# Layer 0 attention: position biases from coefficients and one-hot keys, weighted sums one unit later, short and long products interleaved

## The chip, the cores and the metric

The kernel runs on one core of a Trainium2 chip. The core has a matrix engine (TensorE; PE in the profile, with its weight loads listed as PEld), a vector engine (VectorE, DVE), a scalar engine (ScalarE, ACT), GpSimd (POOL) and SyncE (SP, which issues most transfers). PE writes only to PSUM, which here is eight banks of 128 partitions by 512 float32 numbers. The metric is device time in microseconds (us) of one execution; the time before is 5272.12 us, the median of three runs between 5258.96 and 5286.7.

## The reference

Input x has two images of 128 channels by 256 x 256 pixels, all float32. Two residual layers follow each other, each on group-normalised input (32 groups).

Layer 0 is a halo attention. q, k and v are 1 x 1 convolutions of the normalised x. The image is cut into 32 x 32 windows of 8 x 8 queries; keys and values come from the 12 x 12 pixels around the window. There are 4 heads of 32 channels. The part that the change is about is the position bias and the mask:

```
attn = einsum('bnd,bmd->bnm', q, k) + rel_pos_emb(q, rel_height, rel_width) + FIXED_MASK
attn = softmax(attn); out = einsum('bnm,bmd->bnd', attn, v); x = x + W_out(out)
```

rel_pos_emb is the product of a query with a table row that depends on the horizontal distance to the key, plus the product with one that depends on the vertical distance. FIXED_MASK is minus infinity wherever the horizontal or the vertical distance has the wrong parity, so a query sees only the 6 x 6 keys of its 12 x 12 that match in the parity of row and column.

Layer 1 is a convolution block (a 5 x 1 full convolution, a 3 x 1 depthwise one, a product with a small 1 x 3 dilated one). The change does not touch it.

## The kernel before

`attention_fast` does layer 0, `convolutions_fast` layer 1. Because of the mask the kernel splits pixels by parity. A strip k is eight image rows of one image (64 strips: 2 images x 32), a unit u = 2k + r is one row parity r of a strip (128 units). Within a unit c is the column parity. A unit has 16 pairs of neighbouring windows per column parity; a pair n has 32 queries, and its keys are ten columns by six rows, 60 keys, of which the left window uses the first six columns and the right window the last six.

A unit does this, with the functions' names and lines:

- `normalise(k)` (L199): once per strip, for the next strip: POOL copies two carried rows (L213), DVE normalises two halves into the tile f_xn (L220), in two alternating buffers.
- `queries` (L244): two products of 512 columns into a bank of the two-bank pool f_pj, copied out by ACT to f_q (L253). `keys` (L227): the same into f_kt (L240), with a POOL copy of two carried rows (L232).
- `values` (L255): for four groups j of four pairs, eight products of 128 x 60 weights (60 cells of f_xn) by 128 columns into one f_pj bank; two copies each to f_vt (L268), on DVE but for two of the eight, which go to ACT. f_vt has a 33rd column of ones, for the denominators.
- `scores` (L273): in four banks, one per head. Eight lanes (4 heads x 2 column parities) are 32-row by 60-column pieces of the array. Per lane come 8 products with f_rw (horizontal table, one per query column v; 64 columns each), 4 with f_rh (vertical, one per query row t; 128 columns) and 16 with f_kt (one per pair; 32 columns). All are issued through one helper, L286.
- `numerators` (L302): eight ACT exponentials of 256 columns (L307), two per head, with the mask of a window as bias.
- `attend(u, half)` (L313): 64 products per half, of 60 x 32 weights (numerators) by 33 columns (values), into the banks f_o. `head_outputs` (L327): DVE reciprocals (L332), scaling (L333), transpose (L337).
- `project(u, half)` (L340): one product of 512 columns, two DVE additions of x (L350); after the second half a POOL transfer to memory (L356) and two statistics for layer 1 (L93).

PE's order is written out by hand (the block `manual_schedule`). For each unit it is: scores(u), values(u+1), project(u-1, both halves), attend(u, 0), queries(u+1), keys(u+1), attend(u, 1). The other engines' orders are set by a planner from dependencies. Each float32 product shows in the profile as two LDWEIGHTS and two MATMUL records, so a unit's 224 + 32 + 2 + 128 + 4 = 390 products are 780 MATMUL records.

The reciprocals of the whole layer are kept in `rc_all` (4096 numbers per partition), and `in_range` (L556) takes their largest and smallest after layer 0, to choose a slower fallback if a denominator is out of range. The fallback doesn't run here.

Of the kernel before, what the change touches and what calls it, by code (L numbers as in the profile page):

```python
# [18 lines left out]
P = 128  # L19
W = 256  # L20
HEADS = 4
# [5 lines left out]
XC = 130  # L27
XW = 272

DEN_LOW, DEN_HIGH = 1.0e-24, 1.0e36  # L30

# [14 lines left out]
def host_constants():  # L46
# [16 lines left out]
    mask = np.full((2, 64, 2), NEG, np.float32)  # L63
    for key in range(60):
        c = key // 6
        mask[:, key, 0] = 0.0 if c < 6 else NEG
        mask[:, key, 1] = 0.0 if c >= 4 else NEG

    sel = np.zeros((4, 32, P), np.float32)
    for ch in range(P):  # L70
# [7 lines left out]
        "c_mask": mask.reshape(P, 2),  # L78
# [48 lines left out]
def attention_fast(tc, io, x1_d, norm, st_x, st_y, tags, rc_all):  # L127
# [6 lines left out]
    with ExitStack() as l0:  # L134
# [12 lines left out]
        mask = cload("mask", io["c_mask"], [P, 2])  # L147
        rw = cload("rw", io["rw"], [P, 8, 60])
        rh = cload("rh", io["rh"], [P, 4, 60])
# [13 lines left out]
        sc = [ps_s.tile([P, 512], F32, tag=f"s{h}", name=f"f_s{h}") for h in range(HEADS)]  # L163
        for i in range(2):
            nc.gpsimd.memset(xn[i], 0.0)
            for r in range(2):
                nc.gpsimd.memset(kt[r][i], 0.0)
            nc.gpsimd.memset(vt[i], 1.0)
        for h in range(HEADS):
            nc.vector.memset(sc[h], 0.0)  # L170

        with ExitStack() as setup:
            sp = setup.enter_context(tc.tile_pool(name="f_setup", bufs=6))
            for s in range(NS):
                t = sp.tile([P, 8, W], F32, tag="sx", name=f"f_sx_0_{s}")
                nc.sync.dma_start(t, x[0, :, 8 * s : 8 * s + 8, :])
                norm.chunk(st_x[0], 4 * s, t)
# [5 lines left out]
        raws, norms, qs, pts, ots, x1s, po = {}, {}, {}, {}, {}, {}, {}  # L183
# [43 lines left out]
        def keys(u):  # L227
            k, r = divmod(u, 2)
            s = k % NS
            cur, prev, xt = kt[r][k % 2], kt[r][(k + 1) % 2], xn[k % 2]  # L230
            if s > 0:
                nc.gpsimd.tensor_copy(cur[:, :, :, 0:2], prev[:, :, :, 4:6])  # L232
            for c in range(2):
                for lo, hi in ((0, 2), (2, 6)) if s == 0 else ((2, 6),):
                    n = hi - lo
                    pk = ps_pj.tile([P, 512], F32, tag="pj", name=f"f_pk_{u}_{c}_{lo}")
                    nc.tensor.matmul(  # L237
                        pk[:, : n * P], wkT, xt[:, r, c, 1:129, lo:hi], start=True, stop=True
                    )
                    nc.scalar.copy(  # L240
                        cur[:, c, 1:129, lo:hi], pk[:, : n * P].rearrange("p (j i) -> p j i", i=n)
                    )

        def queries(u):  # L244
# [3 lines left out]
            for c in range(2):  # L248
# [6 lines left out]
        def values(u):  # L255
            k, r = divmod(u, 2)
            xt = xn[k % 2]
            for j in range(4):
                pv = ps_pj.tile([P, 512], F32, tag="pj", name=f"f_pv_{u}_{j}")
                for n in range(4):  # L260
                    for c in range(2):
                        col = 8 * (4 * j + n)
                        nc.tensor.matmul(  # L263
                            pv[64 * c : 64 * c + 60, P * n : P * n + P],
                            xt[:, r, c, col : col + 10].rearrange("p j i -> p (j i)"), wvT, start=True, stop=True,
                        )
                for c in range(2):
                    (nc.scalar.copy if c and j > 1 else nc.vector.tensor_copy)(  # L268
                        vt[u % 2][64 * c : 64 * c + 60, 4 * j : 4 * j + 4, :, 0:32],
                        pv[64 * c : 64 * c + 60].rearrange("p (n h d) -> p n h d", n=4, h=HEADS),  # L270
                    )

        def scores(u):  # L273
            k, r = divmod(u, 2)
            q = qs.pop(u).rearrange("p c (n v t) -> p c n v t", n=NPAIR, v=8)
            lanes = [(h, c) for h in range(HEADS) for c in range(2)]

            def lane(h, c):
                return (
                    sc[h][64 * c : 64 * c + 60].rearrange("p (n v t) -> p n v t", n=NPAIR, v=8),  # L280
                    q[32 * h : 32 * h + 32, c],
                    slice(32 * h, 32 * h + 32),
                )

            def mm(out, w, m, start, stop):
                nc.tensor.matmul(out, w, m, start=start, stop=stop, skip_group_check=True)  # L286

            for v in range(8):
                for h, c in lanes:
                    o, m, rows = lane(h, c)  # L290
                    mm(o[:, :, v], rw[rows, v, :], m[:, :, v], v == 0, False)
            for t in range(4):
                for h, c in lanes:
                    o, m, rows = lane(h, c)
                    mm(o[:, :, :, t], rh[rows, t, :], m[:, :, :, t], False, False)
            for n in range(NPAIR):
                for h, c in lanes:
                    o, m, rows = lane(h, c)
                    keys_n = kt[r][k % 2][rows, c, 8 * n : 8 * n + 10].rearrange("p j i -> p (j i)")
                    mm(o[:, n], keys_n, m[:, n], False, n == NPAIR - 1)  # L300

        def numerators(u):  # L302
            p = wk.tile([P, HEADS, 512], F32, tag="p", name=f"f_p_{u}")
            pts[u] = p
            for h in range(HEADS):
                for e in range(2):
                    nc.scalar.activation(  # L307
                        p[:, h].rearrange("p (n e q) -> p n e q", e=2, q=16)[:, :, e],
                        sc[h].rearrange("p (n e q) -> p n e q", e=2, q=16)[:, :, e],
                        AF.Exp, bias=mask[:, e : e + 1],  # L310
                    )

        def attend(u, half):  # L313
            for c in range(2):
                po[c] = ps_o.tile([P, 8, 33], F32, tag=f"o{c}", name=f"f_o_{u}_{half}_{c}")
            p, v = pts[u], vt[u % 2]
            for n in range(8):
                m = 8 * half + n
                for c in range(2):
                    rows = slice(64 * c, 64 * c + 60)  # L320
                    for h in range(HEADS):
# [3 lines left out]
                        )  # L325

        def head_outputs(u, half):  # L327

            on = wk.tile([P, 2, 8, 32], F32, tag="on", name=f"f_on_{u}_{half}")
            for c in range(2):  # L330
                rc = rc_all[:, 2 * (2 * u + half) + c]
# [4 lines left out]
            ot = wk.tile([P, 512], F32, tag=f"ot{half}", name=f"f_ot_{u}_{half}")  # L336
            nc.vector.transpose(ot, on.rearrange("p c n d -> p (c n d)"))  # L337
            ots[u, half] = ot

# [20 lines left out]

        load_rows(0)
        load_rows(1)
        with tc.manual_schedule(engines={PE}):
            normalise(0)
            keys(0)
            queries(0)
            values(0)
            for u in range(NU + 1):
                k, r = divmod(u, 2)
                b, s = divmod(k, NS)  # L370
                if u < NU:
                    if r == 0:
                        if k + 2 < NB * NS:
                            load_rows(k + 2)
                        if k + 1 < NB * NS:
                            normalise(k + 1)
                    scores(u)
                    numerators(u)
                    if b + 1 < NB and s + 1 < NS:
                        stats_chunk(b + 1, 2 * s + r)  # L380
                        if u < 2:
                            stats_chunk(b + 1, 2 * NS - 2 + u)
                if u + 1 < NU:
                    values(u + 1)
                if u > 0:
                    project(u - 1, 0)
                    project(u - 1, 1)
                if u < NU:
                    attend(u, 0)
                    head_outputs(u, 0)  # L390
                    if u + 1 < NU:
                        queries(u + 1)
                        keys(u + 1)
                    attend(u, 1)
                    head_outputs(u, 1)
                    del pts[u]
# [133 lines left out]
def kernel_body(tc, io, out):  # L530
# [3 lines left out]
    with ExitStack() as ctx:  # L534
# [12 lines left out]
        rc_all = glob.tile([P, 8 * NB * NS, 8, 1], F32, tag="rc_all", name="rc_all")  # L547
        attention_fast(tc, io, x1_d, norm, st_x, st_y, tags, rc_all)
        good = in_range(tc, glob, rc_all)
# [6 lines left out]
def in_range(tc, glob, rc_all):  # L556

    nc = tc.nc
    with ExitStack() as ctx:
        sp = ctx.enter_context(tc.tile_pool(name="f_range", bufs=1))  # L560
        ps = ctx.enter_context(tc.tile_pool(name="f_range_ps", bufs=1, space=PSUM))
        flat = rc_all.rearrange("p a b c -> p (a b c)")
        ends = sp.tile([P, 2], F32, tag="ends", name="ends")
        nc.vector.tensor_reduce(ends[:, 0:1], flat, AX.X, ALU.max)
        nc.vector.tensor_reduce(ends[:, 1:2], flat, AX.X, ALU.min)
        nc.vector.tensor_scalar(ends[:, 0:1], ends[:, 0:1], 1.0 / DEN_LOW, None, ALU.is_le)
        nc.vector.tensor_scalar(ends[:, 1:2], ends[:, 1:2], 1.0 / DEN_HIGH, None, ALU.is_ge)
# [571 lines left out]
```

## Time and profile before

| what | us |
|---|---|
| median of three runs | 5272.12 |
| profiled execution, its own time | 5269.7 |
| its span, first to last instruction | 5267.7 |
| PE, records' busy time (share of the span) | 4224.9 (80%) |
| DVE / ACT / POOL busy | 2252.3 / 1168.6 / 785.9 |
| first and last start of a score product (L286) | 110.4 and 3843.2 |
| layer 1 | about 3880 to the end |

The page of the profile gives one execution. The busy share is a union of records: a matmul's record covers more time than it keeps the array, so PE is not working at its peak when it is busy. The granted clock is the share of PE's full clock that was let through. The groups of instructions say for each line how often, how long, and how long the engine was idle just before and what ended that idleness; "issue" there is time in which the engine waited for nothing that the profile shows.

### The profile page before, as it was taken

The page shows a single profiled execution, that of the slowest core. Times are in us where ns is not written, and L with a number is a line of the kernel's source. Part 1 is how long each engine was busy: PE and PEld are TensorE (multiplying, and loading weights), DVE is VectorE, ACT ScalarE, POOL GpSimd, SP SyncE. Part 2 cuts the span into 40 slices and gives each one's busy share as a digit, 9 for nine tenths or more (in the row PEclk, how much of TensorE's full clock was granted, in tenths as well). Part 3 has the DMA queues.
Part 4 walks back from the last instruction along what each step waited for, and adds up shares of the span by engine and source line. Part 5 has one row for each costly group of instructions (what it writes and reads, how often), then busy time and mean ns, then how long its engine had stood idle before and what let it go on. Part 6 is the DMA issues. An engine that isn't in the chain of part 4 may idle for free. (4 is left out here: it accounts for less than half of the span.)

```text
span 5267.7 us, 218868 instructions
## 1 busy us (share of the span) xinstructions
PE 4224.9 (80%) x104494; PEld 2681.7 (51%) x104494; DVE 2252.3 (43%) x3705; ACT 1168.6 (22%) x2197; POOL 785.9 (15%) x656
## 2 busy tenths in 40 slices
PE   2777777777777777777777777777779999999998
PEld 1555555555555555555555555555533333333333
DVE  8754343333433343334343333344344444444443
ACT  0222222222222222222222222222212222222221
POOL 1000000000000000000000000000023333333333
PEclk9777877787777787877778777877789999999999
DMA  8531111111111111111111111111022222222221
GB/s 337 187 110 40 43 41 52 39 43 39 54 39 44 37 53 39 43 39 53 39 43 40 53 39 43 39 53 40 21 75 97 105 102 96 96 96 98 106 99 70
DMA packets 71458, 367.06 MB, mean 70 GB/s; under 512 B 8224, under 2 KB 8992, under 8 KB 50080
## 3 DMA queue, kind: packets, MB, share of 16 engines
q1 hardware_dynamic: 42912, 218.74, 12.7%
q0 software_dynamic: 27648, 134.23, 6.2%
q8 instruction: 822, 13.47, 1.1%
q14 instruction: 76, 0.62, 0.0%
HBM read 218.72 MB, written 134.22 MB: 67 GB/s over the span
## 5 line engine op out<-in xcount | busy, mean ns | idle before, releaser
L268 DVE COPY f_vt<-f_pv 60x512 f32<-60x512 f32 x768 | 527.4, 687 | 1768.3 <-PE f_pv L263 1759.4
L490 PE MATMUL a<-xm,w 128*128 128x512 f32 (+1 forms) x2560 | 1128.6, 594 | 0.0
L286 PE MATMUL f_s<-f_q,f_kt 32*60 32x32 f32 x32768 | 526.2, 265 | 381.3 <-issue 381.3
L263 PE MATMUL f_pv<-f_wqkvT,f_xn 128*60 128x128 f32 x8192 | 767.5, 359 | 64.6 <-DVE f_vt L268 49.2
L490 PEld LDWEIGHTS a<-xm,w 128*128 128x128 f32 x2560 | 471.2, 188 | 653.6 <-issue 653.0
L307 ACT ACTIVATE f_p<-f_s,f_mask 128x256 f32<-128x256 f32 x1024 | 388.1, 488 | 1826.0 <-PE f_s L286 1826.0
L263 PEld LDWEIGHTS f_pv<-f_wqkvT,f_xn 128*60 128x60 f32 x8192 | 675.2, 184 | 134.2 <-PE f_pv L263 72.5
L286 PEld LDWEIGHTS f_s<-f_q,f_kt 32*60 32x60 f32 x32768 | 501.5, 176 | 414.5 <-issue 414.0
L509 DVE SCALAR_TENSOR_TENSOR t<-t,w,t 128x2048 f32<-128x2048 f32 x128 | 323.2, 2525 | 751.0 <-ACT t L494 738.7
L356 POOL DMA_DIRECT2D f_x<-f_x x128 | 91.3, 713 | 2991.5 <-DVE f_x L350 2991.5
L286 PE MATMUL f_s<-f_q,f_rw 32*60 32x64 f32 x16384 | 266.3, 260 | 297.9 <-issue 297.9
L322 PEld LDWEIGHTS f_o<-f_vt,f_p 60*32 60x32 f32 x32768 | 303.2, 105 | 237.3 <-issue 137.8
L286 PEld LDWEIGHTS f_s<-f_q,f_rw 32*60 32x60 f32 x16384 | 226.9, 151 | 321.7 <-issue 316.4
L286 PE MATMUL f_s<-f_q,f_rh 32*60 32x128 f32 x8192 | 315.6, 407 | 70.3 <-issue 70.3
L322 PE MATMUL f_o<-f_vt,f_p 60*32 60x33 f32 x32768 | 334.5, 201 | 41.0 <-issue 39.3
L494 ACT COPY t<-a 128x512 f32<-128x512 f32 (+1 forms) x256 | 149.4, 583 | 900.6 <-PE a L490 880.2
L347 PE MATMUL f_py<-f_ot,f_woT 128*128 128x512 f32 x512 | 286.8, 651 | 46.6 <-ACT f_vt L268 35.8
L286 PEld LDWEIGHTS f_s<-f_q,f_rh 32*60 32x60 f32 x8192 | 234.9, 180 | 98.7 <-issue 97.9
L237 PE MATMUL f_pk<-f_xn,f_wqkvT 128*128 128x512 f32 (+1 forms) x528 | 266.4, 625 | 4.4 <-issue 3.1
L350 DVE TENSOR_TENSOR f_x<-f_py,f_raw 128x256 f32<-128x256 f32 x512 | 193.5, 420 | 154.0 <-PE f_py L347 152.7
L268 ACT COPY f_vt<-f_pv 60x512 f32<-60x512 f32 x256 | 148.6, 580 | 488.4 <-DVE f_vt L268 488.4
L253 ACT COPY f_q<-f_pq 128x512 f32<-128x512 f32 x256 | 149.8, 586 | 477.3 <-PE f_pq L250 477.3
(93 smaller groups left out, 3122.5 us busy)
## 6 DMA issues: line engine op xcount, KB each, us to landing
f_raw<-in_x SPq DMA_DIRECT2D x62, 1280.0 KB, 6.8
f_x<-f_x POOLq DMA_DIRECT2D x128, 512.0 KB, 5.3
out<-y POOLq DMA_DIRECT2D x64, 1024.0 KB, 4.5
raw<-f_x SPq DMA_DIRECT2D x64, 640.0 KB, 4.2
f_sx<-in_x SPq DMA_DIRECT2D x32, 1024.0 KB, 12.2
f_sx<-in_x SPq DMA_DIRECT2D x64, 512.0 KB, 3.8
raw<-f_x SPq DMA_DIRECT2D x62, 384.0 KB, 4.8
f_raw<-in_x SPq DMA_DIRECT2D x2, 1024.0 KB, 5.7
```

Source lines behind the costliest of these rows:

```text
L237: nc.tensor.matmul(pk[:, : n * P], wkT, xt[:, r, c, 1:129, lo:hi], start=True, stop=True)
L253: nc.scalar.copy(q[:, c, :], pq)
L263: nc.tensor.matmul(pv[64 * c : 64 * c + 60, P * n : P * n + P], xt[:, r, c, col : col + 10].rearrange("p j i -> p (j i)"), wvT, start=True ...
L268: (nc.scalar.copy if c and j > 1 else nc.vector.tensor_copy)(vt[u % 2][64 * c : 64 * c + 60, 4 * j : 4 * j + 4, :, 0:32], pv[64 * c : 64 * ...
L286: nc.tensor.matmul(out, w, m, start=start, stop=stop, skip_group_check=True)
L307: nc.scalar.activation(p[:, h].rearrange("p (n e q) -> p n e q", e=2, q=16)[:, :, e], sc[h].rearrange("p (n e q) -> p n e q", e=2, q=16)[: ...
L322: nc.tensor.matmul(po[c][32 * h : 32 * h + 32, n, :], p[rows, h, 32 * m : 32 * m + 32], v[rows, m, h, :], start=True, stop=True,)
L347: nc.tensor.matmul(py, woT, ots.pop((u, half)), start=True, stop=True)
L350: nc.vector.tensor_tensor(x1[:, :, cols], py[:, 256 * c : 256 * c + 256].rearrange("p (m t) -> p t m", t=4), raws[k][:, r:8:2, cols], ALU.add,
L490: nc.tensor.matmul(pa[:, : n * W], w1[:, tap, :], xt[:, j - 2 + tap : j - 2 + tap + n, 2 : 2 + W], start=tap == 0, stop=tap == 4,)
L494: nc.scalar.copy(t1[:, j : j + n, :].rearrange("p r w -> p (r w)"), pa[:, : n * W])
L509: nc.vector.scalar_tensor_tensor(t3, t1[:, tap : tap + 8, :], w3[:, tap : tap + 1], t3, ALU.mult, ALU.add)
```

## The change

- **Biases.** The tables f_rw and f_rh go. Instead a product per query position (t2, t1) of the strip computes, straight from f_xn, for each head 18 numbers per query: its product with the six or twelve rows of the tables that its keys can need. The weights `wb` for this are made once, from W_q and the tables (`g_rel`). ACT copies the numbers to the tile f_cf, and with them two numbers per query that select its window's mask. Then one product per head and column parity, with the constant one-hot weights `hot` (32 x 64) and 512 columns of f_cf, adds to every score the horizontal term, the vertical term and the mask. So 8 products of 512 columns per unit (`biases`) and 16 products of 128 columns per strip (`coefficients`) stand where 96 products per unit of 64 or 128 columns stood.
- **Exponentials.** The mask is in the scores, so `numerators` goes: four exponentials of 512 columns per unit.
- **Sixty-four keys.** Score and value products take 64 cells instead of 60 (the last four are masked), XC grows to 131, and a value group is copied in one instruction of 128 partitions, always by ACT.
- **Order.** The weighted sums of unit u-1 are now computed during unit u, and the projections follow them. `scores` is split by heads in two passes of 16 parts of 4 products; `values`, `attend`, `coefficients` return lists of parts too, and `merge` lays a list of parts of long products between the parts of short ones. In a unit: biases, scores of heads 0 and 1 with values group 0 and the next unit's queries between them; attend half 0 of u-1 with a projection, values group 1 and coefficients; scores of heads 2 and 3 with values group 2 and keys; attend half 1 with a projection, values group 3 and coefficients.
- **Range check.** Largest and smallest reciprocal are taken per strip, so the two reductions over 4096 numbers become 128 over 64 numbers and two over 64.

```diff
+    hot = np.zeros((HEADS, 32, 64), np.float32)
+    for key in range(64):
+        j, i = divmod(key, 6)
...
+        hot[:, 18, key] = 0.0 if j < 6 else NEG
+        hot[:, 19, key] = 0.0 if 4 <= j < 10 else NEG
...
-        rw = cload("rw", io["rw"], [P, 8, 60])
-        rh = cload("rh", io["rh"], [P, 4, 60])
+        hot = cload("hot", io["c_hot"], [P, 64])
+        keep = cload("keep", io["c_keep"], [P, 4])
...
+        def coefficients(k, t2):
+            if t2 == 0:
+                cfs[k] = wk.tile([P, 2, 2, 512], F32, tag="cf", name=f"f_cf_{k}")
+            cf = cfs[k].rearrange("p r c (n e b t) -> p e b t (r c n)", e=2, b=4, t=4)
+            bank = []
+            def part(t1):
+                if t1 == 0:
+                    bank.append(ps_pj.tile([P, 512], F32, tag="pj", name=f"f_pa_{k}_{t2}"))
+                pa = bank[0]
+                nc.tensor.matmul(
+                    pa[:, P * t1 : P * t1 + P], wb[:, t2, t1].rearrange("p h x -> p (h x)"),
+                    xn[k % 2][:, :, :, 1 + t2 : 129 : 4, 1 + t1], start=True, stop=True,
+                )
+                if t1 == 3:
+                    for e in range(2):
+                        nc.scalar.activation(
+                            cf[:, e, t2], pa.rearrange("p (t m e) -> p e t m", t=4, e=2)[:, e],
+                            AF.Identity, bias=keep[:, 2 * e + 1 : 2 * e + 2],
+                            scale=keep[:, 2 * e : 2 * e + 1],
+                        )
+            return [lambda t=t: part(t) for t in range(4)]
...
+        def biases(u):
+            k, r = divmod(u, 2)
+            for h in range(HEADS):
+                rows = slice(32 * h, 32 * h + 32)
+                for c in range(2):
+                    nc.tensor.matmul(
+                        sc[h][64 * c : 64 * c + 64, :], hot[rows, :], cfs[k][rows, r, c, :],
+                        start=True, stop=False, skip_group_check=True,
+                    )
...
+            def part(n):
+                for h in heads:
+                    rows = slice(32 * h, 32 * h + 32)
+                    for c in range(2):
                         nc.tensor.matmul(
+                            sc[h][64 * c : 64 * c + 64, 32 * n : 32 * n + 32],
+                            keys_k[rows, c, 48 * n : 48 * n + 64], qs[u][rows, c, 32 * n : 32 * n + 32],
+                            start=False, stop=n == NPAIR - 1, skip_group_check=True,
                         )
...
+                if n == NPAIR - 1:
...
+                    for h in heads:
+                        nc.scalar.activation(pts[u][:, h], sc[h], AF.Exp)
...
+        def merge(small, large):
+            done = 0
+            for i, f in enumerate(small):
+                f()
+                upto = (i + 1) * len(large) // len(small)
+                for g in large[done:upto]:
+                    g()
+                done = upto
+            for g in large[done:]:
+                g()
...
-                    scores(u)
-                    numerators(u)
...
+                if now:
+                    biases(u)
+                    merge(scores(u, 0), values(u, 0) + (queries(u + 1) if u + 1 < NU else []))
+                merge(
+                    attend(u - 1, 0) if last else [],
+                    ([lambda: project(u - 2, 1)] if u > 1 else []) + (values(u, 1) if now else [])
+                    + (coefficients(k + 1, 2 * r) if more else []),
+                )
+                if now:
+                    merge(scores(u, 1), values(u, 2) + (keys(u + 1) if u + 1 < NU else []))
+                    del qs[u]
+                merge(
+                    attend(u - 1, 1) if last else [],
+                    ([lambda: project(u - 1, 0)] if last else []) + (values(u, 3) if now else [])
+                    + (coefficients(k + 1, 2 * r + 1) if more else []),
+                )
...
-        flat = rc_all.rearrange("p a b c -> p (a b c)")
...
+        nc.vector.tensor_reduce(span[:, 0:1], ends[:, 0, :], AX.X, ALU.max)
+        nc.vector.tensor_reduce(span[:, 1:2], ends[:, 1, :], AX.X, ALU.min)
```

## The prediction

> **What bounds the kernel now.** I read the page first (busy shares, slices, queues), then the waits between 500 and 3700 us, then one unit in the timeline, then that unit by stages.
>
> ```profile
> PE 4224.9 (80%) x104494; PEld 2681.7 (51%) x104494; DVE 2252.3 (43%) x3705; ACT 1168.6 (22%) x2197; POOL 785.9 (15%) x656
> PEclk9777877787777787877778777877789999999999
> q8 instruction: 822, 13.47, 1.1%
> ...
> PE f_s L286 <- issue: 637.7, 382, 4.3
> PE f_o L322 <- issue: 39.3, 15, 4.6
> PE f_pv L263 <- DVE f_vt L268: 34.1, 88, 0.6
> ```
>
> PE is busiest, no other engine is near half. In layer 0 its clock is 0.7 to 0.8, in layer 1 full. Between 500 and 3700 us, some 110 units, its long waits end with "issue": no engine and no transfer is waited for. The queue line says what it is. 822 fetches of 16.4 KB (13.47 MB / 822) carry the 209 thousand PE instructions, one per 254. The single records agree: in the score stage PE stops after every 256 instructions, 1.4 to 2.3 us each time. Example: a fetch starts at 2002.36, takes 1.31 us, and PE resumes at 2005.04; the next one starts 1.1 us after that. So a new block of 256 cannot be had sooner than about 3.5 us after the last one was entered, and PE waits where it eats a block faster.
>
> ```profile
> 2032.43 1.86 PE L286 MATMUL f_s<-f_q,f_rw 32*60 32x64 f32 x103 [2.06 <-issue]
> ...
> 2039.64 1.99 PE L286 MATMUL f_s<-f_q,f_kt 32*60 32x32 f32 x128 [0.71 <-issue]
> 2043.12 0.89 PE L286 MATMUL f_s<-f_q,f_kt 32*60 32x32 f32 x42 [1.48 <-issue]
> 2043.94 6.35 PE L263 MATMUL f_pv<-f_wqkvT,f_xn 128*60 128x128 f32 x64
> 2050.70 2.16 PE L347 MATMUL f_py<-f_ot,f_woT 128*128 128x512 f32 x4 [0.41 <-ACT f_vt L268]
> 2052.79 1.29 PE L322 MATMUL f_o<-f_vt,f_p 60*32 60x33 f32 x128
> 2054.01 1.99 PE L250 MATMUL f_pq<-f_xn,f_wq_s 128*128 128x512 f32 x4
> 2055.87 2.02 PE L237 MATMUL f_pk<-f_xn,f_wqkvT 128*128 128x512 f32 x4
> 2057.82 1.29 PE L322 MATMUL f_o<-f_vt,f_p 60*32 60x33 f32 x128
> ```
>
> The bracket is the idle time before a row: 128 records (256 instructions with their weight loads) last 2 us and then PE stands still. The long products have no such gap.
>
> ```profile
> 2029.90:2043.90 14.00, 8.70 (x458) 7.80 (x448) 3.38 (x7) 0.00 (x0) 0.85 (x1) 0.57 0.02 5
> 2043.90:2050.70 6.80, 6.39 (x70) 5.69 (x64) 3.81 (x6) 3.60 (x9) 0.00 (x0) 0.63 0.01 2
> 2050.70:2052.80 2.10, 2.10 (x6) 0.61 (x6) 1.07 (x3) 0.58 (x1) 0.00 (x0) 1.00 0.00 0
> 2052.80:2054.00 1.20, 1.20 (x129) 1.16 (x128) 1.07 (x3) 0.00 (x0) 0.05 (x1) 1.00 0.05 14
> 2054.00:2057.80 3.80, 3.80 (x16) 1.34 (x8) 2.58 (x7) 1.76 (x3) 0.66 (x1) 1.00 0.34 138
> 2057.80:2059.00 1.20, 1.20 (x129) 1.18 (x128) 0.00 (x0) 0.61 (x1) 0.41 (x1) 1.00 0.05 14
> ```
>
> Stages of one unit: scores, values, projection, attend, queries and keys, attend; after the length the busy times of PE, PEld, DVE, ACT and POOL, then the clock. A unit lasts 29.1 us. Scores take half of it with PE idle 38% of the time, and the clock falls to half there; the values that follow start at half clock, though they never pause. Value records start 55 ns apart at full clock and 107 at half.
>
> **The change, part by part, per unit, on PE's path.** I add what each part will take at full clock, from the starts of single records.
>
> Handovers come first, as the new order is made of them. Before, groups of different array shape meet six times a unit; after, 56 times (merge lays 6, 9, 6, 9 long parts among 16, 8, 16, 8 short ones; neighbours of one kind join). Long to short: the last 512-column record starts 0.53 us before the first attend record, and 0.43 of that is its own stream, so 0.10. Short to long: 0.123 us from the last attend record to the first query record; 0.213 from the last score record to the first value record, seen at half clock only. Between 0.12 and 0.21 I take 0.17 for scores.
>
> - Biases: the 96 products with f_rw and f_rh (192 records) go. Eight products of 512 columns come, 16 records of 0.43 us over eight lanes. The f_rw records at full clock start 7 to 10 ns apart, where one such stream is 53 ns, so eight lanes do run side by side: 2 x 0.43, 0.95 with fill (1.8 if only four do).
> - Scores: 256 records as before, but a pass has two heads, four lanes. A lane repeats every 0.100 us at half clock (its 60-column weight load), so 0.053 at full. A block of three parts, six records per lane, takes 0.05 + 5 x 0.053 + 0.17 = 0.50; one of two parts 0.39. Eight and four of them: 5.6 (4.9 to 6.2). That is more than the 2.5 of 256 records at 9.7 ns in one go.
> - Values: 16 parts of four records, starts spread over 0.163, then 0.107 + 0.10 to hand over: 0.37 each, 5.9 (5.1 to 6.7); 6.8 now.
> - Attend: 16 parts of 16 records, spread 0.093 to 0.12, plus 0.123: 0.24 each, 3.8 (3.5 to 4.3); 2.4 now.
> - Queries, keys, projections: six products, 2 x 0.43 + 0.10 = 0.96 each, 5.8; 5.9 now.
> - Coefficients, new: eight products of 128 columns. Two records of 0.107, and a handover of 0.10: 0.31. They read every 24th number of f_xn; f_rh, which reads every fourth, starts 28.5 ns apart at both clocks, that is 0.228 per record and lane, so up to 0.55. I take 0.40: 3.2 (2.5 to 4.4).
>
> Sum 0.95 + 5.6 + 5.9 + 3.8 + 5.8 + 3.2 = 25.3 us against 29.1.
>
> Fetching: 310 products are 1240 instructions, 4.84 blocks where 390 made 6.1; at 3.5 us that is 17 us, below 25. The densest stretch, scores with values, has 56 instructions in 0.87 us, a block in 4.0 us, so the 6.3 us of issue waits per unit (637.7 + 39.3 + 11.6 over 110) should go. If the parts were faster than I think, 17 plus the 5.8 of the 24 instructions that are nearly free of fetching, 22.4, is a floor.
>
> The Trainium skill, "Runtime: NRT & Kernel Launch", Instruction fetch mechanics, says that crossing a 16 KiB boundary is mostly hidden. By that rule the 6.3 us of pauses would have another cause and would stay, and the unit would take 25.3 + 6.3 = 31.6 us, 5580 in all; the trace shows them at every 256th instruction, and the sum goes by the trace.
>
> The clock: layer 0 stands at 0.79 from 500 to 3700 us. It falls in stretches with pauses (0.57 in the scores, PE busy 8.70 of 14.00) and stands at 1.00 in the attend stages, short records without pauses, and in the long products. The new unit has long products every microsecond and no pause over 0.2, so I take full clock.
>
> The Trainium skill, "TensorE: Matmul & The Clock Gate", Part 1, puts the half clock after an idle window of some 3.4 us. The waits here are mostly 1 to 2 us and the clock falls all the same; by the page's rule pauses of this length cost no clock, filling them would win none, and with today's share of half clock the unit would take 30.6 us.
>
> What lies beside PE:
>
> - ACT now per unit: exponentials four of 512 (eight of 0.38 were 3.0; now 2.4 to 3.0), copies of q, k and values 8 x 0.59 = 4.7, coefficients 4 x 0.48 = 1.9: about 9.5 of 25. The tightest place: the second query copy stands behind two exponentials, ready 1.2 us after its product; values group 1 needs that bank 1.4 us after. If that slips, 0.5 us twice a unit. Should the new function need table loads among the exponentials, four of 1.28 us fit into ACT's free time.
> - DVE loses six copies (4.1 us). normalise now waits for values of the unit before (f_xn's buffer is read longer), 2.7 us of DVE; coefficients need it only after the first score pass, some 7 us later. Behind it on DVE stand the projection's additions, whose bank is free for 2.4 us more.
> - POOL and SP: same transfers in the loop; rows are loaded two strips ahead. At the start 360 KB of tables go and about 120 KB come, under 1 us at 337 GB/s. wb's fill (POOL) and 36 small ACT copies lie beside 98 us of DVE statistics.
> - Ends: the two reductions over 4096 (4.4 us each) stand before layer 1 and go: -8.8. Unit 0 has no attend, the last one's follow after the loop as now; the first coefficients replace the first values. Together about -10.
>
> Total: 5269.7 - 128 x 3.8 - 10 = 4773; the profiled execution stands 2.4 below the median. Predicted 4770.
>
> **Rivals.**
>
> - *Half clock stays (slower).* Array streams double, handovers partly: biases 1.8, scores 8, values 7.5, attend 4.5, long products 10.8, coefficients 5, so about 38. With a share h of half clock a unit takes 25.3 + 12.7 h; it is slower from h = 0.30, and with today's 0.42 it is 30.6, 5450 us. For it: scores with array pieces of 32 rows are weak work, and handovers leave the array empty for some 6 us a unit. Against: the attend stages keep full clock.
> - *Handovers cost more.* At 0.40 a pair instead of 0.25, 28 x 0.15 = 4.2 eats all the gain: 29.5, 5310. Nothing in the trace shows pieces as short as these. It decides at 0.39 a pair.
> - *Fetch or bank waits remain*, two us a unit: 5030.
> - *Everything at its low end*, the fetch floor of 22.4: 4400.
> - *The change does nothing:* PE bound by fetching with the same blocks. The block count alone falls by a fifth; I give it little.
>
> **How the numbers follow.** Forecast (4590 to 4960) 0.47; low ends 0.13; remaining waits (up to 5245) 0.16; within 0.5% (26 us, about what a measurement here can tell from nothing) 0.03; the two slower rivals together 0.21. Range: 4430 leaves out about 0.06 below, 5400 some 0.12 above.
>
> **What would show it.** Right: no "issue" row over 100 us in the waits of 500 to 3700, clock above 0.95 there, a unit (one distance of equal records) of 24 to 27 us, no table loads in the loop. Wrong: clock still at 0.8; value parts more than 0.45 us long; PE waiting for f_pv or f_pq copies by ACT, or for f_cf; score rows with issue gaps.

## The result and the profile after

The changed kernel takes 6282.45 us (median of four runs, 6263.94 to 6296.79) against 5271.61 for the kernel before: 1.191 times as long, 95% interval 1.187 to 1.196. The forecast was 4770 with a range of 4430 to 5400, so it has the wrong sign and the time lies outside the range.

The page of the profile after (busy shares, clock by slices, queues) and the waits of PE from 500 to 4500 us:

```profile
span 6261.9 us, 177334 instructions
PE 6036.0 (96%) x84022; PEld 3082.1 (49%) x84022; DVE 1792.6 (29%) x3061; ACT 1535.1 (25%) x2493; POOL 740.6 (12%) x657
PEclk8777776677767676677677767767777999999999
q8 instruction: 661, 10.83, 0.7%
...
PE f_s L352 <- ACT f_cf L316: 74.8, 52, 1.5
PE pv_x L127 <- DVE q_x L125: 1.3, 1, 1.3
PE f_pv L335 <- DVE f_x L431: 0.7, 1, 0.7
PE f_s L367 <- issue: 0.5, 1, 0.5
```

The first things to see are what came true. PE is busy 96% of the span; the "issue" wait of the score products went from 637.7 us (500 to 3700) to 0.5 (500 to 4500); the fetches fell from 822 to 661. And still the kernel is 1000 us slower. What is left to explain it stands in the clock row: in layer 0 the digits are 6 and 7 where they were 7 and 8. Layer 1 still has nines and lasts as long as before (1420 us from the start of the last score record to the end of the span, 1424 before).

The timeline of PE over the second half of one unit and the start of the next, and the three stages that it runs through (length, then busy times of PE, PEld, DVE, ACT and POOL, then the clock):

```profile
2510.24 0.29 PE L392 MATMUL f_o<-f_vt,f_p 64*32 64x33 f32 x16
2510.46 0.84 PE L310 MATMUL f_pa<-f_xn,f_wb 128*128 128x128 f32 x2
2511.23 0.29 PE L392 MATMUL f_o<-f_vt,f_p 64*32 64x33 f32 x16
...
2512.45 1.46 PE L310 MATMUL f_pa<-f_xn,f_wb 128*128 128x128 f32 x4
...
2515.37 0.70 PE L335 MATMUL f_pv<-f_wqkvT,f_xn 128*64 128x128 f32 x4
2516.00 0.65 PE L367 MATMUL f_s<-f_q,f_kt 32*64 32x32 f32 x16
...
2522.46 2.07 PE L273 MATMUL f_pk<-f_xn,f_wqkvT 128*128 128x512 f32 x2
...
2513.80:2525.90 12.10, 12.10 (x154) 6.71 (x153) 0.50 (x1) 3.98 (x8) 0.00 (x0) 0.58 0.01 1
2525.90:2533.10 7.20, 7.20 (x155) 3.88 (x154) 1.99 (x8) 1.38 (x3) 0.65 (x1) 1.00 0.02 5
2533.10:2541.10 8.00, 8.00 (x183) 4.62 (x182) 0.61 (x2) 3.98 (x7) 0.00 (x0) 1.00 0.01 2
```

A coefficient product (f_pa, two records of 128 columns) holds PE 0.77 us from its start to the next short part, more than twice a value part, though it has half its records. Behind the coefficients comes the score pass, and the first one of the three stages, a pass of heads 2 and 3 with values and keys, ran at a clock of 0.58 and took 12.1 us; the pass of heads 0 and 1 of the next unit found full clock and took 7.1, biases included (2533.14 to 2540.25; the third window runs on into the next stage). There is no pause in either.

Adding up single records from 500 to 4500 us (one unit is 37.2 us there) gives each part's time, at full clock and as it ran:

| part, per unit | forecast | at full clock | as it ran |
|---|---|---|---|
| biases | 0.95 | 0.91 | 1.52 |
| scores, 8 blocks of three and 4 of two | 5.6 | 5.30 | 7.77 |
| values, 16 | 5.9 | 5.90 | 7.62 |
| attend, 16 | 3.8 | 3.57 | 3.69 |
| queries, keys, projections, 6 | 5.8 | 6.34 | 9.98 |
| coefficients, 8 | 3.2 | 5.85 | 6.59 |
| sum | 25.3 | 27.9 | 37.2 |

The unit of 37.2 us is the distance from the first score record to the last, divided by 127. "At full clock" is the number of parts times the median of those that ran wholly at full clock. The third column has 8.6 us more from half clock and 0.7 of waiting for f_cf (in the coefficients' row). So the handovers were priced well, the coefficients were not, and the clock does most of the rest.

### The profile page after: what moved, and what is told of

Same layout as the page of the kernel before. It is cut to its first block, busy times and chain, and to the rows that moved or that the text cites. A ratio compares the mean times of both kernels' runs of the same rounds, so it can differ in the third digit from the quotient of the medians.

```text
span 6261.9 us, 177334 instructions
## 1 busy us (share of the span) xinstructions
PE 6036.0 (96%) x84022; PEld 3082.1 (49%) x84022; DVE 1792.6 (29%) x3061; ACT 1535.1 (25%) x2493; POOL 740.6 (12%) x657
## 5 line engine op out<-in xcount | busy, mean ns | idle before, releaser
L367 PEld LDWEIGHTS f_s<-f_q,f_kt 32*64 32x64 f32 x32768 | 930.0, 193 | 830.1 <-issue 830.0
L335 PE MATMUL f_pv<-f_wqkvT,f_xn 128*64 128x128 f32 x8192 | 1119.6, 361 | 0.7 <-DVE f_x L431 0.7
L367 PE MATMUL f_s<-f_q,f_kt 32*64 32x32 f32 x32768 | 1100.3, 274 | 0.5 <-issue 0.5
L392 PEld LDWEIGHTS f_o<-f_vt,f_p 64*32 64x32 f32 x32768 | 380.2, 109 | 1015.3 <-issue 1013.5
L310 PE MATMUL f_pa<-f_xn,f_wb 128*128 128x128 f32 x2048 | 802.7, 515 | 0.0
L392 PE MATMUL f_o<-f_vt,f_p 64*32 64x33 f32 x32768 | 610.8, 209 | 3.8 <-issue 3.2
L335 PEld LDWEIGHTS f_pv<-f_wqkvT,f_xn 128*64 128x64 f32 x8192 | 489.9, 164 | 107.8 <-issue 2.7
L316 ACT ACTIVATE f_cf<-f_pa,f_keep 128x256 f32<-128x256 f32 x512 | 343.3, 769 | 753.5 <-PE f_pa L310 753.5
L292 PE MATMUL f_pq<-f_xn,f_wq_s 128*128 128x512 f32 x512 | 414.7, 902 | 0.0
L310 PEld LDWEIGHTS f_pa<-f_xn,f_wb 128*128 128x128 f32 x2048 | 363.7, 209 | 61.7 <-ACT f_q L295 0.6
```

What stands on the lines that cost most here:

```text
L292: nc.tensor.matmul(pq, wq_s, xn[k % 2][:, r, c, 1:129, 1:5], start=True, stop=True)
L310: nc.tensor.matmul(pa[:, P * t1 : P * t1 + P], wb[:, t2, t1].rearrange("p h x -> p (h x)"), xn[k % 2][:, :, :, 1 + t2 : 129 : 4, 1 + t1], ...
L316: nc.scalar.activation(cf[:, e, t2], pa.rearrange("p (t m e) -> p e t m", t=4, e=2)[:, e], AF.Identity, bias=keep[:, 2 * e + 1 : 2 * e + 2 ...
L335: nc.tensor.matmul(pv[64 * c : 64 * c + 64, P * n : P * n + P], xt[:, r, c, o : o + 64], wvT, start=True, stop=True,)
L367: nc.tensor.matmul(sc[h][64 * c : 64 * c + 64, 32 * n : 32 * n + 32], keys_k[rows, c, 48 * n : 48 * n + 64], qs[u][rows, c, 32 * n : 32 * ...
L392: nc.tensor.matmul(po[c][32 * h : 32 * h + 32, n, :], p[rows, h, 32 * m : 32 * m + 32], v[rows, m, h, :], start=True, stop=True,)
```

## The experiments

The first theory was "clock": score passes with only short pieces and value parts are too weak to hold full clock. The rival was "handovers": 56 changes of array shape a unit cost more than they seemed. Clock below is the granted clock from 500 to 3000 us.

| run | time, us | ratio to before | unit, us | clock | coefficient record to next, us |
|---|---|---|---|---|---|
| before | 5271.61 | | 29.4 | 0.78 | |
| changed kernel | 6282.45 | 1.191 | 37.2 | 0.71 | 0.307 |
| e1 spread order | 6191.02 | 1.177 | 36.7 | 0.71 | 0.307 |
| e2 grouped order | 5370.96 | 1.021 | 30.2 | 0.80 | 0.307 |
| e3 products added | 7388.18 | 1.404 | 46.1 | 0.67 | 0.307 |
| e4 contiguous copy | 5235.87 | 0.995 | 29.3 | 0.89 | 0.112 |
| e5 copy, 16 bytes apart | 5866.00 | 1.117 | 33.8 | 0.79 | 0.228 |
| e6 contiguous, spread | 5130.38 | 0.977 | 28.4 | 0.89 | 0.112 |
| e7 contiguous, grouped | 4768.17 | 0.908 | 25.5 | 0.90 | 0.112 |
| e8 contiguous, spread, runs of four | 4582.75 | 0.873 | 24.1 | 0.96 | 0.112 |
| e9 contiguous, each product twice | 5345.87 | 1.009 | 30.0 | 0.93 | 0.112 |
| e10 as e8, without the copy | 5246.10 | 0.991 | 29.2 | 0.85 | 0.307 |
| e11 as e8, coefficients first | 4472.79 | 0.845 | 23.2 | 0.98 | 0.112 |

Ratios are against runs of the kernel before made beside each kernel; its medians there lie between 5248.70 and 5294.89. Unit is the distance from the first score record to the last, divided by 127.

**e1, order of the long parts.**

```diff
+        def spread(v, full):
+            if len(full) != 2:
+                return full + v
+            return [full[0], v[0], v[1], full[1], v[2], v[3]]
...
-                    merge(scores(u, 0), values(u, 0) + (queries(u + 1) if u + 1 < NU else []))
+                    merge(scores(u, 0), spread(values(u, 0), queries(u + 1) if u + 1 < NU else []))
...
-                    merge(scores(u, 1), values(u, 2) + (keys(u + 1) if u + 1 < NU else []))
+                    merge(scores(u, 1), spread(values(u, 2), keys(u + 1) if u + 1 < NU else []))
```

> The changed kernel with one edit of order: in the two score passes of a unit the long parts stand as query, value, value, query, value, value (and so with keys) where they stood as four values and then two queries. Same products, same 56 handovers. Theory 'clock': the changed kernel's parts add up to 28 us a unit at full clock and it takes 37 because the score passes with only values in them are too weak to hold the clock; a query product in every 3 us lifts them, the share of half clock from 500 to 4500 us falls from 0.58 to under 0.25, and the time to 5200-5600. Rival 'handovers': the short pieces cost this whatever their neighbours, time stays at 6280 within 60.

6191.02 us, ratio 1.177 (1.173 to 1.181), clock 0.71 as before the edit. Neither came out: the time fell by 90 us, not by 700, and the clock did not come back. So a score pass that begins with four value parts and no query or key product isn't what drops it.

**e2, no interleaving.**

```diff
-                upto = (i + 1) * len(large) // len(small)
+                upto = 0
```

> The changed kernel with merge laying all short parts first and the long ones behind them: 56 handovers a unit become 8. Theory 'handovers': some 48 x 0.2 to 0.27 us of a unit go, 37 becomes 24 to 27, 4650-5000. Theory 'clock': 48 handovers at full clock are worth 6 us, but passes of 256 instructions in a row bring pauses for instructions back (up to 1.8 us, three or four times a unit) and with them some half clock: 26 to 31 us a unit, 4900-5500, issue waits over 200 us.

5370.96 us, ratio 1.021 (1.018 to 1.024): 7.0 us a unit less than the changed kernel, inside the range that "clock" had given; but issue waits stayed at 12 us, far below the 200 expected. Instead the coefficient products wait for the copies of the values, 156.4 us between 500 and 3700, some 1.5 a unit. The clock rose to 0.80. Interleaving so finely costs more than the pauses that it hides, but handovers and clock change together here, and the run doesn't separate them.

**e3, strong products added to the score passes.**

```diff
                 pv = bank[0]
+                for e in range(2 if j % 2 == 0 else 0):
+                    nc.tensor.matmul(
+                        pv[:, P * n : P * n + P], wkT, xn[k % 2][:, r, e, 1:33, 1:5],
+                        start=True, stop=True,
+                    )
```

> The changed kernel with work added: ahead of each of the eight value parts in the score passes two products of 128 columns that the part overwrites (their result is not used), 16 products a unit more. Theory 'clock': the stretch gets stronger work and keeps full clock, so more work takes less time: 28 + 8 x 0.6 = 33 us a unit, 5600-5900, half clock under 0.25. Rival 'handovers': 8 x 0.6 to 1.1 us more a unit, 6900-7400.

7388.18 us, ratio 1.404 (1.400 to 1.409). The theory as I had put it fell here: more strong work in the score pass did not hold the clock, which went down to 0.67. The time lies in the range that the rival "handovers" had given, at its upper end, so this run by itself speaks for the rival. The windows before the falls of the clock give another theory. Each stay at one clock lasts a multiple of 3.41 us. In the changed kernel the clock fell from full to half 183 times between 500 and 4500 us, and all 183 times the window just before held four or more coefficient records; there were 220 such windows at full clock. So the clock falls in the coefficients, and the score pass inherits it.

**e4, the coefficients' numbers laid side by side.**

```diff
+            for t2 in range(4):
+                nc.vector.tensor_copy(
+                    xq[:, t2].rearrange("p t (m j) -> p t m j", j=32),
+                    cells[:, :, 1 + t2 : 129 : 4, 1:5].rearrange("p m j t -> p t m j"),
+                )
...
-                    xn[k % 2][:, :, :, 1 + t2 : 129 : 4, 1 + t1], start=True, stop=True,
+                    xq[:, t2, t1], start=True, stop=True,
```

> The changed kernel with a copy of f_xn laid out by query position (four DVE copies of 512 columns a strip), so that the coefficient products read 128 neighbouring numbers. If the stride is what makes a coefficient record 0.43 us apart from the next, it falls to 0.11 and a part from 0.77 to 0.31-0.40: 3 us less a unit, 5850-5950, clock hardly changed. If not, no change: 6280.

5235.87 us, ratio 0.995 (0.994 to 0.996): 1047 us less than the changed kernel, and the clock went up to 0.89, which I had not expected. (The 0.43 us in the expectation was a misreading: the record is 0.307 us from the next in the changed kernel.) The timeline of PE in this run, at the same place as above:

```profile
2521.85 0.29 PE L398 MATMUL f_o<-f_vt,f_p 64*32 64x33 f32 x16
2522.07 0.49 PE L316 MATMUL f_pa<-f_xq,f_wb 128*128 128x128 f32 x2
2522.49 0.29 PE L398 MATMUL f_o<-f_vt,f_p 64*32 64x33 f32 x16
...
2523.36 0.71 PE L316 MATMUL f_pa<-f_xq,f_wb 128*128 128x128 f32 x4
```

The part takes 0.42 us instead of 0.77. Per unit the coefficients give back 2.8 us (6.59 to 3.77); all other parts together 5.1 (30.6 to 25.5), without a change to any of them. Between 500 and 3700 us 15 of 72 falls of the clock now follow a window with coefficients. The cost of the strided read was thus about one third direct and two thirds clock.

**e5, the same copy with gaps.** The copy is written and read with every fourth number, 16 bytes apart.

```diff
-                    xq[:, t2, t1], start=True, stop=True,
+                    spaced(t2, t1), start=True, stop=True,
```

> The kernel with the laid-out copy, but in the copy the 128 numbers of one coefficient product lie every fourth number apart (16 bytes; 96 bytes in the changed kernel, 4 bytes in the copy of the run before). Theory 'a record pays for every 16 bytes it touches': a record is again 0.43 us from the next, the strong stretch before the score pass is weak again, half clock back above 0.5, 6200-6300. Rival 'only the long distance or the many levels of the pattern hurt': as the contiguous copy, 5200-5300.

5866.00 us, ratio 1.117 (1.109 to 1.126), between the two ranges given. A record is 0.228 us from the next: 0.112 at 4 bytes, 0.228 at 16, 0.307 at 96. 0.228 is what the f_rh products of the kernel before show at the same distance (28.5 ns x 8 lanes). Clock and time go with it: 0.89, 0.79, 0.71 and 29.3, 33.8, 37.2 us a unit.

The Trainium skill, "SBUF — State Buffer", Door 1 (its note on cachelines), says that reads which stay in a 16-byte line go at full rate and that each new line costs extra, so four float32 numbers can share it. The runs agree that 4 bytes are nearly free (0.112 us against the 0.107 of the bare stream) and 16 cost twice the time. Read that way, 96 bytes, also one line per number, would cost no more than 16, and it measured 0.307 against 0.228. The 96-byte read also has more levels in its pattern than the copy with gaps; the runs don't separate distance from pattern there.

**e6, contiguous and spread.** The copy of e4 with the order of e1.

> Contiguous copy and the spread order of the score passes together. Theory 'a window of 3.4 us that keeps the array too empty drops the clock for what follows': the parts of the contiguous run add up to 25 us a unit at full clock plus 1.3 of waits, it took 29.3 with a half-clock share of 0.23; with a query or key product among the first parts of each pass the share falls under 0.12, 27-28 us a unit, 4930-5080. Rival 'the order did nothing in the first test and does nothing here': 5236 within 40.

5130.38 us, ratio 0.977 (0.975 to 0.979): 105 us less than e4, 28.4 us a unit, a smaller gain than I expected; half clock 0.20 of the time, not 0.12. The order helps a little once the stride is gone.

**e7, contiguous and grouped.**

> Contiguous copy, short parts first and long ones behind them, 8 handovers a unit instead of 56. The parts without handovers add up to about 20 us at full clock. Theory 'handovers are worth 0.1 to 0.13 us each and pauses for instructions come back where 256 instructions stand in a row': 20 + 4 to 6 us, 4700-5000, issue waits over 200 us. If pauses don't come back: 4400.

4768.17 us, ratio 0.908 (0.906 to 0.910). 25.5 us a unit against 29.3 with 56 handovers and the same copy, at nearly the same clock (0.90 and 0.89): 48 handovers fewer are worth 3.8 us net, about 0.08 each. Two waits work against them, some 1 us a unit for instructions (97.8 us at f_o and 22.7 at f_pv between 500 us and the end of layer 0) and 1.4 us a unit of the coefficient products for the copies of the values (160.9 us), so a handover by itself is worth more than that; the 0.1 to 0.13 expected is possible and not shown.

**e8, runs of four short parts.**

```diff
-                upto = (i + 1) * len(large) // len(small)
+                upto = (i + 1) * len(large) // len(small) if i % 4 == 3 else done
```

> Contiguous copy, spread order, and short parts laid in runs of four (64 to 128 instructions) between the long ones: 24 handovers a unit instead of 56, no run of 256 instructions. 32 handovers at 0.12 us are 3.9 us a unit less than the run with contiguous copy and spread order: 23 to 25 us, 4400-4700. If the handovers cost nothing beyond their place, no better than that run.

4582.75 us, ratio 0.873 (0.871 to 0.875), 24.1 us a unit, as expected, but not by handovers alone: the parts at full clock add up to 21.7 us where they made 25.0 in e6, so 32 handovers fewer are worth about 3.3 us, 0.10 each; the other 1.0 comes with the clock, 0.96 where it was 0.89. Issue waits are about 60 us between 500 us and the end of layer 0. Between grouped and fully interleaved lies the better order: runs short enough that no block of 256 instructions is eaten at once, long enough that handovers are few.

**e9, length or strength.** The contiguous copy, but every coefficient product is issued twice.

```diff
-                nc.tensor.matmul(
+                for _ in range(2):
+                  nc.tensor.matmul(
                     pa[:, P * t1 : P * t1 + P], wb[:, t2, t1].rearrange("p h x -> p (h x)"),
```

> Contiguous copy, and every coefficient product issued twice into the same columns: as long a stay as with numbers 16 bytes apart (a part 0.64 us there, 0.42 + 0.22 here), but with the array full. Theory 'the strided read empties the array and that drops the clock': half clock stays at 0.15-0.25 and a unit costs only the added 8 x 0.22 = 1.8 us, 31 us, 5400-5500. Rival 'the length of the stretch between the score passes matters, not its strength': half clock 0.43, 33.8 us a unit as with 16 bytes, 5800-5900.

5345.87 us, ratio 1.009 (1.007 to 1.012), 30.0 us a unit, even below the 31 (and 5400) of the theory. Stages from 500 to 3000 us in the changed kernel, in e5 and in e9, in that order (the clock is the third figure from the right):

```profile
500.00:3000.00 2500.00, 2451.50 (x41608) 1332.66 (x41604) 532.82 (x1217) 633.56 (x1079) 128.77 (x166) 0.71 0.10 34
```

```profile
500.00:3000.00 2500.00, 2425.87 (x46166) 1360.78 (x46170) 719.57 (x1960) 700.99 (x1198) 179.09 (x186) 0.79 0.12 37
```

```profile
500.00:3000.00 2500.00, 2418.83 (x53709) 1500.69 (x53710) 776.64 (x1700) 784.16 (x1355) 200.66 (x210) 0.93 0.13 43
```

PE is busy for 97 to 98% in all three. The timelines have one coefficient part each, first e5, then e9, with the short part behind it:

```profile
2510.47 0.70 PE L322 MATMUL f_pa<-f_xq,f_wb 128*128 128x128 f32 x2
2511.10 0.29 PE L404 MATMUL f_o<-f_vt,f_p 64*32 64x33 f32 x16
```

```profile
2501.24 0.71 PE L317 MATMUL f_pa<-f_xq,f_wb 128*128 128x128 f32 x4
2501.89 0.29 PE L399 MATMUL f_o<-f_vt,f_p 64*32 64x33 f32 x16
```

A coefficient part lasts 0.63 us in e5 and 0.64 in e9; in the one it is two records, 0.228 us apart, in the other four that are 0.112 apart. The clock is 0.79 in the first and 0.93 in the second. So it is not how long the coefficients take. From 500 to 3000 us 54 of 78 falls in e5 follow a window with coefficients, in e9 none of 37. What the run leaves open is whether the clock follows the fullness of the array or the mere number of records and weight loads, since e9 doubles these too.

A count over the windows answers that. As an estimate of how full the array is, take for each record its columns times 0.83 ns (128 columns in 0.107 us) times the part of the array that it uses (rows x columns of 128 x 128), and add this up over each window of 3.41 us at full clock, from 500 to 3000 us, in all 13 kernels. Of 467 windows under 0.30, 445 were followed by a fall of the clock; of 2555 between 0.30 and 0.50, 407; of 3380 at 0.50 or more, none. The number of records tells much less: of the 467 windows with the fewest, 198 were followed by a fall. Windows with four or more coefficient records hold 0.33 in the changed kernel, 0.37 in e5, 0.45 in e4 and 0.54 in e9.

**e10, the good order with the strided read.**

> The fastest version so far without its contiguous copy: f_xn is read at 96 bytes again, order spread, runs of four short parts. Theory 'strided read': a coefficient part is 0.35 us longer (2.8 a unit) and the clock falls again, half-clock share over 0.3 against 0.06: 30-33 us a unit, 5300-5700. Rival 'the order holds the clock by itself': 24.05 + 2.8 = 27 us, 4900-5000.

5246.10 us, ratio 0.991 (0.989 to 0.993), 29.2 us a unit: between both. Against e8 the coefficients cost 3.0 us directly (5.97 against 2.96) and the other parts 2.1 more, with the clock down from 0.96 to 0.85. The order softens the fall and doesn't prevent it.

**e11, coefficients ahead of values.**

```diff
-                    ([lambda: project(u - 1, 0)] if last else []) + (values(u, 3) if now else [])
-                    + (coefficients(k + 1, 2 * r + 1) if more else []),
+                    ([lambda: project(u - 1, 0)] if last else [])
+                    + (coefficients(k + 1, 2 * r + 1) if more else []) + (values(u, 3) if now else []),
```

> The fastest version so far with the coefficient parts ahead of the value parts in both attend passes, so that the bias products, which wait 1.5 us for the last coefficients once a strip (80 us in 3200), find them ready. If that wait goes and nothing takes its place: 0.7 us a unit less, 4480-4510. If the long products ahead of it only move the wait: 4570-4590.

4472.79 us, ratio 0.845 (0.844 to 0.847), 7 us below the range expected and the fastest version. Waits of PE in it, 500 to 3000 us:

```profile
PE f_s L373 <- issue: 30.2, 18, 3.0
PE f_o L398 <- issue: 29.8, 30, 1.6
PE f_s L358 <- ACT f_cf L322: 21.7, 52, 0.4
```

The wait for f_cf, 1.5 us a strip, is down to 0.4; the clock is 0.98.

## Why the prediction was wrong, point by point

- *Pauses for instructions would go*: right. They went from 6.3 us a unit to nothing, and the reading that a block of 256 cannot follow sooner than 3.5 us was good enough to choose the runs of four. (In its example the fetch starts at 2002.60 us and PE resumes at 2005.24, both some 0.2 later than told there; the reading stands.)
- *Handovers*: right in size. Attend, value, score and bias parts came out within 7% of the forecast at full clock (the table), long products at 1.06 instead of 0.96.
- *Coefficients 3.2 (2.5 to 4.4)*: mis-sized; 5.85 at full clock. The upper bound took 0.228 us a record from f_rh, whose numbers lie 16 bytes apart; at 96 bytes it is 0.307, and the part is 0.77 instead of at most 0.55. The nearest row was no bound: the new read has six times its distance, and its pattern has more levels.
- *"The new unit has long products every microsecond and no pause over 0.2, so I take full clock"*: this step failed, and it gave the sign. I had read the fall of the clock in the kernel before as the work of pauses. The changed kernel has none, and the clock was lower than ever. The coefficient products are long and strong by their shape; read with gaps they leave the array mostly empty (a record takes 0.307 us for 0.107 us of stream), and the falls come there. That is 8.6 of the 37.2 us; without it the unit would have taken about 28.6, less than the 29.4 before.
- *The rival "half clock stays"* named the right term for the loss but another cause (weak score pieces, handovers): by the estimate under e9 the score passes of the changed kernel fill 0.50 of the array at full clock, the attend passes from their first coefficient on 0.27. Its price at the measured share of half clock, 0.58, would have been 25.3 + 12.7 x 0.58 = 32.7 us; the rest of the 37.2 is the coefficients, the wait for f_cf, and 14.8 us instead of 12.7 between full and half clock (8.6 / 0.58). It had got only 0.21, shared with another.
- *Bank and copy waits*: right, none appeared in the changed kernel (they did in e2 and e7). *f_cf late for the biases*: named only as a sign of being wrong; it is real, 0.7 us a unit, and mostly went with e11. The copies to f_cf take 0.77 us each where 0.48 had been counted.
- The Trainium skill's rule in "TensorE: Matmul & The Clock Gate", Part 1, that an idle window throttles PE, had been set beside the kernel before. Here PE is never idle for such a window by its records and the clock falls all the same; the runs speak for a measure of how full the array is, which is inferred from e5, e9 and the counts of windows, not read from a row.

What stays open: there is no sharp level in the estimate, and what decides between 0.30 and 0.50 is not shown; nor is what empties the windows before the remaining falls in e6 and e7, which hold 0.30 and 0.25 (medians). e1 and e3 show that strong work behind the coefficients doesn't bring the clock back quickly. At half clock a product takes twice as long, so it fills a window half as well: by the same estimate the half-clock windows of e3 hold 0.31 on average, with the added products, and those of the changed kernel 0.30. That this is the reason is argued, not shown by a run of its own.

## What to carry to other kernels

A long product is only strong if its moving numbers (the operand that streams past the weights) lie side by side: count the distance in bytes between neighbours of the moving operand before calling its stream free, and lay them out with an engine that has time. Runs of four were enough here: the products added in e3 read four neighbouring numbers and skip 8 bytes, and their records also start 0.112 us apart at full clock. When work is interleaved, ask of every stretch of some 3 us how full it keeps the array, not whether PE has a pause. And interleave as coarsely as the fetching of instructions allows, since each change of array shape costs (some 0.1 us here, e8).

## What the hardware showed that I had not expected

- A float32 record of 128 rows and 128 moving columns starts 0.112 us before the next when the columns lie 4 bytes apart, 0.228 at 16 bytes, 0.307 at 96 (e4, e5, the changed kernel).
- The clock fell to half while PE's records covered 98% of the time (2451.50 of 2500 us in the changed kernel), and 183 of 183 falls followed a window of 3.41 us with four or more strided coefficient records; doubling those products with their numbers side by side raised the clock from 0.89 to 0.93 (e4, e9). No window whose estimated fill was 0.50 or more came before a fall, in any of the 13 kernels.
- Adding 16 products a unit at a place where the clock was already down cost 8.9 us a unit (37.2 to 46.1, e3), and doubling 8 where it was up cost 0.7 (29.3 to 30.0, e9).
